# State space layer: decay tiles made earlier, one copy of B, C and the step rows, and four norm steps and two MLP steps moved to other turns

## The chip, the cores and the metric

The kernel runs on one core of one Trainium2 chip. A core has five engines that work side by side, each through its own queue in order: TensorE (PE, matrix products), VectorE (DVE), ScalarE (ACT), GpSimd (POOL) and SyncE (SP, which here issues transfers). They wait for one another through semaphores. An instruction that waits holds up everything behind it on its own engine. The metric is the time of one execution in microseconds (us) on the device; less is better. The kernel before took 11207.35 us in the median of three runs (11202.88 to 11211.71).

## The reference

The program is a network of four layers, each of a mixer and a feed-forward part. The change lies in the mixer of the third layer, a state space (Mamba) block followed by a small MLP. For an image of 4 x 64 x 128 x 128 values the reference computes, cut to what matters:

```python
mu = mean(xf); var = mean(square(xf - mu))
xn = (xf - mu) * rsqrt(var + LN_EPS)                 # norm over 64 channels
xi, z = split(xn @ in_proj_w.T)                      # 2 x 128 channels
xs = silu(causal_conv4(xi) + conv_b)
x_dbl = xs @ x_proj_w.T                              # 4 step, 16 B and 16 C rows
dt = softplus(x_dbl[..., :4] @ dt_proj_w.T + dt_proj_b)
def step(h, t):                                      # 128 channels x 16 states
    h = exp(dt_t * A) * h + (dt_t * x_t) * B_t
    return h, sum(h * C_t over states)
y = (scan of step) + xs * D
out = (y * silu(z)) @ out_proj_w.T
h1 = gelu(out @ fc1_w.T + fc1_b)                     # 128 -> 512, along the width
result = h1 @ fc2_w.T + fc2_b                        # 512 -> 128
```

## The kernel before, in words

The function `l2_conv` (line 2302) does this layer. The 4 images are taken as 2 pairs; the partitions hold two images of 64 channels, or, in the scan, two states of 64 channels. A sequence of 16384 positions is cut in 32 chunks of 512 positions (`L`, four columns of the image), so that there are 64 chunks in all. A chunk has T = 32 units (two images, 16 tiles of one state pair each). One unit is worked on in one turn of the main loop, and the loop goes over 2048 units in order. For each unit t:

- `decay` (line 2767) makes exp(dt A) on ACT into a tile `da`, three turns ahead; five such tiles exist.
- `spread` (line 2776) is a PE product that copies two rows of B over the partitions into a bank of PSUM, once for two units, three turns ahead, in odd turns t. There are four banks. A bank is used again for the input of the same units, so a spread waits for an earlier scan.
- `inputs` (line 2810) multiplies on DVE, one turn ahead, dt x by the spread B. Units 16 and 17 of every chunk are apart (`APART`): their B comes by a transfer, their product is made on POOL five turns ahead (`inputs_apart`, line 2805), their decay goes to a PSUM bank.
- `one_state` (line 2816) runs the scan over 512 positions on DVE, and the product `gs` with C on POOL.
- `summed` (line 2832) adds the products of two units in PSUM with PE, five turns later.

All else of a chunk is put in by turn numbers. `at(turn, step)` enters a step in a list; in each turn, after the unit's own work, the steps of that turn are issued. The order of issue is the order on PE, ACT, DVE and POOL (`manual_schedule`); SP's order follows from the framework. For chunk n, `norm` counts its turns from T(n-2), `project` from T(n-1), `leave` from T(n+1). So within the 32 turns of one chunk, steps of three other chunks run too, and turn numbers can be compared modulo 32.

- `norm` (line 2478): `scale`, `centre` (PE takes the mean away), `square` (ACT copies the result and squares it), `mean2` (PE sums the squares), `root` (ACT), `newton` (POOL refines the reciprocal root), `back` (PE spreads it, 8 products), `kept` (ACT copies it), `done` (POOL multiplies).
- `project` (line 2549): `conv`, `gate_in`, `silu`, then `bcr` (PE makes B three times, which gives with the products of `minus` a split in three bf16 parts, C, and the four step rows; all in one PSUM tile), `bcr_out` (three copies on ACT), `c_out` (transfers of B and C rows to memory), `steps` (PE, turn 15), `parts` (ACT, turn 16), `exp`, `one_more` (17), `log`, `lost` (18), `size` and `scaled` (POOL), and `twice` (transfers that lay dt and dt x out for the units).
- `leave` (line 2688): `sums` (DVE), `project_out`, `projected`, `layer1`, `hidden`, `gelu`, `layer2`, `put`.

Two PSUM names have one buffer each: `pa` (two banks wide) is shared by the convolution, the gate, B and C, the steps and both halves of layer1; `pn` is shared by the norm's products, project_out and layer2. A step that takes one of these must wait until the step before it has been copied out.

In the code and in the profile the functions and lines are:

Of the kernel before, what the change touches and what calls it, by code (L numbers as in the profile page):

```python
# [22 lines left out]
P = 128  # L23
# [2278 lines left out]
def l2_conv(env, x, out, prm):  # L2302
# [15 lines left out]
    with ExitStack() as ctx:  # L2318
# [7 lines left out]
        def load(name, shape, src):  # L2326
            t = cp.tile(shape, F32, name=name)
            nc.sync.dma_start(t, src)
            return t
# [54 lines left out]
        nc.vector.tensor_scalar(minus_i, env.ident[0 : 2 * N, 0 : 2 * N], -1.0, None, ALU.mult)  # L2384
        both = cp.tile([P, H], F32, name="both")
        nc.vector.tensor_add(both, env.ident[:, 0:H], env.ident[:, H:P])
        dtw = load("dtw", [R, D], prm["dt_proj_wT"])
        dtb = load("dtb", [P, 1], prm["dt_proj_b"].unsqueeze(1))
        am = cp.tile([P, S // 2, 2], F32, name="am")
        for i in range(2):  # L2390
# [27 lines left out]
        def at(turn, *steps):  # L2418
            turns.setdefault(turn, []).extend(steps)
# [4 lines left out]
        def tile_of(box, key, shape, name=None, bufs=2, dt=F32, pool=None):  # L2424
            box[key] = (pool or sb).tile(shape, dt, name=name or key, bufs=bufs)
            return box[key]
# [51 lines left out]
        def norm(n, t0):  # L2478
            g, w0 = chunks[n]
            x_ = boxes[n]  # L2480

            def scale(js):
                r, k = x_["rows"]
                if 0 in js:
                    tile_of(x_, "xn", [P, 3 + L], bufs=3)
                for j in js:
                    nc.scalar.activation(
                        x_["xn"][:, 3 + j * C : 3 + j * C + C], r["xt"][:, k + j, :], AF.Identity,
                        bias=r["nb"][:, k + j : k + j + 1], scale=r["rs16"][:, k + j : k + j + 1],
                    )  # L2490

            def centre():
                nc.tensor.matmul(tile_of(x_, "pm", [P, L], "pn", 1, pool=p1), less, x_["xn"][:, 3:], start=True, stop=True)

            def square():
                nc.scalar.copy(x_["xn"][:, 3:], x_["pm"])
                nc.scalar.activation(tile_of(x_, "sq", [P, L], "sq", 1), x_["pm"], AF.Square)

            def mean2():
                pv = tile_of(x_, "pv", [P, NW, 2], "pn", 1, pool=p1)  # L2500
                for q in range(NW):
                    nc.tensor.matmul(pv[:, q, :], x_["sq"][:, q * C : q * C + C], each, start=True, stop=True)

            def root():
                v, rs = tile_of(x_, "v", [P, NW, 2]), tile_of(x_, "rs", [P, NW, 2])
                nc.scalar.activation(v, x_["pv"], AF.Identity, bias=env.eps5)
                nc.scalar.activation(rs, v, AF.Ln)
                nc.scalar.activation(rs, rs, AF.Exp, scale=-0.5)

            def newton():  # L2510
                v, rs, t = x_["v"], x_["rs"], tile_of(x_, "r2", [P, NW, 2])
                nc.gpsimd.tensor_tensor(t, rs, rs, ALU.mult)
                nc.gpsimd.tensor_tensor(t, t, v, ALU.mult)
                nc.gpsimd.tensor_scalar(t, t, 0.5, -1.5, ALU.mult, ALU.add)
                nc.gpsimd.tensor_tensor(rs, rs, t, ALU.mult)

            def back():
                pr = tile_of(x_, "pr", [P, L], "pn", 1, pool=p1)
                for q in range(NW):
                    for b in range(2):  # L2520
                        nc.tensor.matmul(
                            pr[b * H : b * H + H, q * C : q * C + C], x_["rs"][:, q, b : b + 1].to_broadcast([P, H]),
                            env.ident, start=True, stop=True,
                        )

            def kept():
                nc.scalar.copy(tile_of(x_, "rt", [P, L], bufs=1), x_["pr"])

            def done():
                xn = x_["xn"]  # L2530
                if w0 == 0:
                    nc.gpsimd.memset(xn[:, 0:3], 0.0)
                else:
                    nc.gpsimd.tensor_copy(xn[:, 0:3], boxes[n - 1]["xn"][:, L : L + 3])
                nc.gpsimd.tensor_tensor(xn[:, 3:], xn[:, 3:], x_["rt"], ALU.mult)

            at(t0 - 2, lambda: scale((0, 1)))
            at(t0, lambda: scale((2, 3)))
            at(t0 + 3, centre)
            at(t0 + 4, square)  # L2540
            at(t0 + 5, mean2)
            at(t0 + 6, root)
            at(t0 + 8, newton)
            at(t0 + 11, back)
            at(t0 + 12, kept)
            at(t0 + 13, done)


        def project(n, t0):
# [52 lines left out]
            def bcr_out():  # L2602
                ps = x_["ps"]
                nc.scalar.copy(tile_of(x_, "bt", [3 * N, 2, L], dt=BF16), ps[0 : 3 * N])
                nc.scalar.copy(tile_of(x_, "bc", [2 * N, 2, L], bufs=1), ps[0 : 2 * N])
                nc.scalar.copy(tile_of(x_, "r", [R, 2, L], bufs=1), ps[3 * N : 3 * N + R])

            def c_out():
                for b in range(2):
# [13 lines left out]
            def steps():  # L2623
                pu = tile_of(x_, "pu", [P, 2, L], "pa", 1, pool=pa)
                for b in range(2):
                    nc.tensor.matmul(pu[:, b, :], dtw, x_["r"][:, b, :], start=True, stop=True)

            def parts():
                pu = x_["pu"]
# [58 lines left out]
        def leave(n, t0):  # L2688
# [7 lines left out]
            def project_out(b):  # L2696
                po = tile_of(x_, "po", [P, NW, H], "pn", 1, pool=p1)
                for j in range(NW):
                    nc.tensor.matmul(po[:, j, :], x_["y%d" % b][:, j * C : j * C + C], wo, start=True, stop=True)

            def projected(b):
                nc.scalar.copy(tile_of(x_, "o%d" % b, [P, NW * H], bufs=1), x_["po"].rearrange("c w h -> c (w h)"))

            def layer1(b):
                pf = tile_of(x_, "pf%d" % b, [P, F, NW * H], "pa", 1, pool=pa)
                for k in range(F):
                    nc.tensor.matmul(pf[:, k, :], f1[:, k, :], x_["o%d" % b], start=True, stop=True)  # L2707

            def hidden(b):
                gl = tile_of(x_, "gl%d" % b, [P, F, NW * H], bufs=1)  # L2710
                for k in range(F):
                    nc.scalar.activation(gl[:, k, :], x_["pf%d" % b][:, k, :], AF.Identity, bias=b1[:, k : k + 1])  # L2712
# [24 lines left out]

            at(t0 - S + LAG, lambda: sums(0))
            at(t0 + LAG, lambda: sums(1))
            at(t0 + 9, lambda: project_out(0))  # L2740
            at(t0 + 10, lambda: projected(0))
            at(t0 + 13, lambda: project_out(1))
            at(t0 + 14, lambda: projected(1))
            at(t0 + 18, lambda: layer1(0))
            at(t0 + 19, lambda: hidden(0))
            at(t0 + 21, lambda: layer1(1))
            at(t0 + 22, lambda: hidden(1))
            at(t0 + 24, gelu)
            at(t0 + 28, lambda: layer2(0, 0))
            at(t0 + 29, lambda: layer2(0, 1))  # L2750
# [13 lines left out]
        def apart(t):  # L2764
            return t % T // 2 * 2 in APART

        def decay(t):
            x_, b, s, _ = unit(t)
            da = bank(t, t % 2) if apart(t) else sb.tile([P, L], F32, name="da", bufs=5)
            nc.scalar.activation(da, x_["dt%d" % b][:, s % 2, :], AF.Exp, scale=am[:, s : s + 1])  # L2770
            live["da", t] = da

# [72 lines left out]
        with tc.manual_schedule(engines={E_.PE, E_.Activation, E_.DVE, E_.Pool}):  # L2845
            base_table()
            for n in range(0, len(chunks), NG):
                statistics(n, T * (n - 3))
            for n in range(len(chunks)):
                norm(n, T * (n - 2))  # L2850
                project(n, T * (n - 1))
                leave(n, T * (n + 1))
            for t in range(-4 * T, units + 2 * T):
                if 0 <= t + 3 < units:
                    decay(t + 3)
                if 0 <= t + 3 < units:
                    if (t + 3) % 2 == 0 and not apart(t + 3):
                        spread(t + 3)
                if 0 <= t + 10 < units and t % 2 == 0 and apart(t + 10):
                    fetch_b(t + 10)  # L2860
                if 0 <= t + 5 < units and apart(t + 5):
                    inputs_apart(t + 5)
                if t % QU == 2 and 0 <= t + 6 < units:
                    fetch(t + 6)
                if 0 <= t + 1 < units and not apart(t + 1):
                    inputs(t + 1)
                if 0 <= t < units:
                    one_state(t)
                for step in turns.pop(t, ()):
                    step()  # L2870
                if 0 <= t - LAG < units and (t - LAG) % 2 == 1:
                    summed(t - LAG)
# [697 lines left out]
```

## Time and profile before

| what | value |
|---|---|
| median of three runs | 11207.35 us |
| the profiled execution | 11202.36 us, its span 11200.5 us |
| stretch of the scans, span time 6333 to 10198 us | 3865 us, 64 chunks |
| DVE, POOL, PE, ACT busy in that stretch | 3692, 3508, 3381, 3175 us |
| mean granted TensorE clock in that stretch | 0.89 |
| ACT copies of B and C, of the step rows (L2605, L2606) | 1005 and 1007 ns each |

How to read it: the table by stretches gives for each stretch its length, then the busy time of PE, weight loads, DVE, ACT and POOL (with the number of instructions), the granted clock, the share of the transfer engines and GB/s. A list of waits has engine, tile and line of the one that waits, who released it, the sum in us, how many times, and the longest. The order in time has the start, the length, engine, line, operation, what is written from what, and in brackets the idle time of the engine just before it and what ended it. Starts are in us from the beginning of the span. The page merges neighbouring instructions of one kind (x8 is eight of them).

### The profile page before, as it was taken

The numbers are of one execution on the slowest core, as the hardware profiler recorded it, in microseconds if no ns is written. First come the engines' busy times: TensorE is split into PE (matmuls) and PEld (weight loads), VectorE is DVE, ScalarE is ACT, GpSimd is POOL, SyncE is SP. The second block draws the span as 40 slices with busy tenths as digits, with TensorE's granted clock in tenths as the row PEclk, the third lists the DMA queues.
The fourth block names the chain that finished last, engine by engine and source line by source line (L and its number), as shares of the span: only waits on it lengthen the run. The fifth ranks groups of instructions, "written<-read, shape, count | busy, mean of one in ns | idle before, by whom it ended". The sixth has DMA issues, their size and how long they took to land. (4 is left out here: it accounts for less than half of the span.)

```text
span 11200.5 us, 114412 instructions
## 1 busy us (share of the span) xinstructions
PE 6448.2 (58%) x33010; PEld 3781.1 (34%) x33010; DVE 9431.5 (84%) x14943; ACT 7408.7 (66%) x10451; POOL 5992.4 (54%) x5674
## 2 busy tenths in 40 slices
PE   7777686000000000003999688888888888887665
PEld 5665454000000000002898333333333333334342
DVE  7567646999999999998778599999999999997455
ACT  4244443788886777765555488888888888885443
POOL 1000025899992000001455499999999999894222
PEclk8887798555555555556999789889988989898877
DMA  6312246111111111112111254554554545543534
GB/s 195 107 36 48 56 160 159 51 58 56 59 58 54 57 54 56 53 45 61 47 56 47 70 126 119 127 126 118 131 123 121 128 122 123 129 116 108 193 132 169
DMA packets 806489, 1080.31 MB, mean 96 GB/s; under 512 B 245612, under 2 KB 462927, under 8 KB 792271
## 3 DMA queue, kind: packets, MB, share of 16 engines
q1 hardware_dynamic: 761918, 946.59, 30.6%
q0 software_dynamic: 34368, 124.14, 3.3%
q8 instruction: 266, 4.36, 0.2%
q14 instruction: 385, 3.15, 0.1%
q10 hardware_dynamic: 9552, 2.08, 0.1%
HBM read 699.16 MB, written 255.91 MB: 85 GB/s over the span
## 5 line engine op out<-in xcount | busy, mean ns | idle before, releaser
L2827 POOL TENSOR_TENSOR gs<-hist,cc 128x512 f32<-128x512 f32 x2048 | 2570.8, 1273 | 268.5 <-DVE hist L2822 200.9
L2822 DVE TENSOR_TENSOR_SCAN hist<-da,state,bs 128x512 f32<-128x512 f32 x1860 | 2360.0, 1271 | 48.2 <-ACT da L2770 47.0
L1698 PE MATMUL pm<-ident,m 128*1 128x128 f32 x1 | 0.4, 372 | 3193.0 <-DVE m L1696 3193.0
L2814 DVE TENSOR_TENSOR bs<-dx,bs 128x512 f32<-128x512 f32 x1920 | 1299.3, 677 | 159.9 <-PE bs L2780 110.9
L1506 POOL TENSOR_TENSOR diff<-key 128x2048 f32<-128x2048 f32 (+11 forms) x364 | 1384.0, 3851 | 81.8 <-DVE key L1511 75.5
L2770 ACT ACTIVATE da<-dt,am 128x512 f32<-128x512 f32 x1920 | 1294.5, 715 | 38.2 <-DVE hist L2822 29.7
L2838 PE MATMUL py<-gs,both 128*64 128x512 f32 x4096 | 1212.9, 672 | 1.4 <-POOL gs L2827 1.3
L1698 PEld LDWEIGHTS pm<-ident,m 128*1 128x1 f32 x1 | 0.1, 79 | 3193.1 <-issue 3193.1
L1936 POOL IOTA row<- 72x1 int32 x1 | 0.2, 230 | 1770.4 <-ACTq L1873 1770.4
L1528 ACT COPY keep<-rank 128x1536 int16<-128x1536 int16 (+11 forms) x364 | 612.8, 1686 | 437.7 <-DVE rank L1530 389.0
L1504 ACT COPY low<-key 128x2048 f32<-128x2048 f32 (+11 forms) x364 | 627.7, 1725 | 313.6 <-DVE key L1511 276.5
L1529 DVE COPY_PREDICATED rank<-back,rank 128x1536 int16<-128x1536 uint8 (+11 forms) x364 | 781.7, 2147 | 16.7 <-ACT keep L1528 16.7
L1530 DVE COPY_PREDICATED rank<-back,keep 128x1536 int16<-128x1536 uint8 (+11 forms) x364 | 777.8, 2137 | 12.5
L1511 DVE TENSOR_TENSOR key<-low,key 128x2048 f32<-128x2048 f32 (+11 forms) x364 | 744.5, 2045 | 12.4
L1510 DVE TENSOR_TENSOR key<-low,key 128x2048 f32<-128x2048 f32 (+11 forms) x364 | 749.1, 2058 | 2.4 <-ACT low L1504 2.4
L1507 ACT ACTIVATE turned<-diff 128x2048 int8<-128x2048 f32 (+11 forms) x364 | 600.4, 1699 | 8.4 <-POOL diff L1506 8.4
L1519 ACT ACTIVATE back<-turned 128x3072 uint8<-128x3072 int8 (+12 forms) x182 | 582.5, 3200 | 0.0
L2249 PE MATMUL pe<-ew,xg 128*128 128x128 f32 x4096 | 506.6, 278 | 0.0
L2249 PEld LDWEIGHTS pe<-ew,xg 128*128 128x128 f32 x4096 | 491.0, 193 | 19.2 <-issue 2.9
L1031 POOL DMA_DIRECT2D state<-zz x16 | 18.5, 1156 | 856.2 <-DVE zz L1021 615.8
L2780 PE MATMUL bs<-bt,pick 96*128 96x512 bf16 x960 | 394.5, 411 | 120.0 <-DVE hist L2822 117.5
L2707 PE MATMUL pa<-o,f 128*128 128x256 f32 x1024 | 361.5, 514 | 107.5 <-ACT gl L2712 93.4
(858 smaller groups left out, 17618.0 us busy)
## 6 DMA issues: line engine op xcount, KB each, us to landing
cc<-cd SPq DMA_DIRECT2D x1024, 256.0 KB
xt<-state SPq DMA_DIRECT2D x64, 1024.0 KB
dt<-w SPq DMA_DIRECT2D x512, 128.0 KB
dx<-up SPq DMA_DIRECT2D x512, 128.0 KB
xo<-state SPq DMA_DIRECT2D x128, 256.0 KB
state<-xo POOLq DMA_DIRECT2D x128, 256.0 KB, 3.0
xl<-in_L_ffn_weight SPq DMA_DIRECT2D x32, 1024.0 KB
tk<-in_x SPq DMA_DIRECT2D x32, 512.0 KB
```

Of the source, the lines that this page charges most:

```text
L1504: nc.scalar.copy(c, l)
L1506: nc.gpsimd.tensor_sub(d, lo[part], hi[part])
L1510: nc.vector.tensor_tensor(lo[part], c, hi[part], ALU.min)
L1511: nc.vector.tensor_tensor(hi[part], c, hi[part], ALU.max)
L1529: nc.vector.copy_predicated(l, t, h)
L1530: nc.vector.copy_predicated(h, t, kv)
L2249: T.matmul(w["pe"][:, j, :], w["xg"][:, q, j, :], ew[:, q, :], start=False, stop=(j == 3 and q == E - 1))
L2770: nc.scalar.activation(da, x_["dt%d" % b][:, s % 2, :], AF.Exp, scale=am[:, s : s + 1])
L2814: nc.vector.tensor_mul(live["db", t], x_["dx%d" % b][:, s % 2, :], live["bs", t - s % 2])
L2822: nc.vector.tensor_tensor_scan(h, live.pop(("da", t)), live.pop(("db", t)), 0.0 if first else state[b][:, s : s + 1], ALU.mult, ALU.add,)
L2827: nc.gpsimd.tensor_tensor(gs, h, live.pop(("cc", t)), ALU.mult)
L2838: nc.tensor.matmul(x_["py%d" % b][h * H : h * H + H], both, live.pop(("gs", t - 1 + h)), start=False, stop=(s == S - 1),)
```

## The change

It does six things.

1. The tile pool of decays has eight tiles instead of five, and a decay is issued five turns ahead instead of three. The two units apart stay at three.
2. `bcr_out` makes two copies instead of three. The tile `bc` takes all 100 rows of the PSUM tile (B three times and the four step rows, where it took 64), and `r` is gone.
3. The weights of `steps` are laid out for those 100 rows: `dtw` has 96 rows of zeros, written by DVE, above its four. `steps` contracts over 100 rows instead of 4.
4. In `norm`: `square` goes from turn 4 to 5, `mean2` from 5 to 9, `root` from 6 to 10, `newton` from 8 to 12, `back` from 11 to 13, `kept` from 12 to 14, `done` from 13 to 16.
5. In `leave`: the two `project_out` go from turns 9 and 13 to 11 and 15, the two `projected` from 10 and 14 to 12 and 16.
6. In `leave`: the two `layer1` go from turns 18 and 21 to 17 and 20, the two `hidden` from 19 and 22 to 18 and 21.

```diff
-        dtw = load("dtw", [R, D], prm["dt_proj_wT"])
+        dtw = cp.tile([3 * N + R, D], F32, name="dtw")
+        nc.vector.memset(dtw, 0.0)
+        nc.sync.dma_start(dtw[3 * N :], prm["dt_proj_wT"])
...
-            at(t0 + 4, square)
-            at(t0 + 5, mean2)
-            at(t0 + 6, root)
-            at(t0 + 8, newton)
-            at(t0 + 11, back)
-            at(t0 + 12, kept)
-            at(t0 + 13, done)
+            at(t0 + 5, square)
+            at(t0 + 9, mean2)
+            at(t0 + 10, root)
+            at(t0 + 12, newton)
+            at(t0 + 13, back)
+            at(t0 + 14, kept)
+            at(t0 + 16, done)
...
-                nc.scalar.copy(tile_of(x_, "bc", [2 * N, 2, L], bufs=1), ps[0 : 2 * N])
-                nc.scalar.copy(tile_of(x_, "r", [R, 2, L], bufs=1), ps[3 * N : 3 * N + R])
+                nc.scalar.copy(tile_of(x_, "bc", [3 * N + R, 2, L], bufs=1), ps[0 : 3 * N + R])
...
-                    nc.tensor.matmul(pu[:, b, :], dtw, x_["r"][:, b, :], start=True, stop=True)
+                    nc.tensor.matmul(pu[:, b, :], dtw, x_["bc"][:, b, :], start=True, stop=True)
...
-            at(t0 + 9, lambda: project_out(0))
-            at(t0 + 10, lambda: projected(0))
-            at(t0 + 13, lambda: project_out(1))
-            at(t0 + 14, lambda: projected(1))
-            at(t0 + 18, lambda: layer1(0))
-            at(t0 + 19, lambda: hidden(0))
-            at(t0 + 21, lambda: layer1(1))
-            at(t0 + 22, lambda: hidden(1))
+            at(t0 + 11, lambda: project_out(0))
+            at(t0 + 12, lambda: projected(0))
+            at(t0 + 15, lambda: project_out(1))
+            at(t0 + 16, lambda: projected(1))
+            at(t0 + 17, lambda: layer1(0))
+            at(t0 + 18, lambda: hidden(0))
+            at(t0 + 20, lambda: layer1(1))
+            at(t0 + 21, lambda: hidden(1))
...
-            da = bank(t, t % 2) if apart(t) else sb.tile([P, L], F32, name="da", bufs=5)
+            da = bank(t, t % 2) if apart(t) else sb.tile([P, L], F32, name="da", bufs=8)
...
-                if 0 <= t + 3 < units:
+                if 0 <= t + 5 < units and not apart(t + 5):
+                    decay(t + 5)
+                if 0 <= t + 3 < units and apart(t + 3):
                     decay(t + 3)
```

## The prediction

> **What bounds the kernel now.** I read the page, the table by stages, the waits of each engine in the state space stage, and then one group of 32 turns (span time 7545 to 7604 us) engine by engine in order of time.
>
> ```profile
> span 11200.5 us, 114412 instructions
> 6333.00:10198.00 3865.00, 3380.72 (x13418) 1432.78 (x13417) 3692.49 (x4336) 3175.37 (x4769) 3508.41 (x3504) 0.89 0.50 123
> DVE bs L2814 <- PE bs L2780: 110.9, 100, 3.0
> DVE hist L2822 <- ACT da L2770: 48.0, 54, 3.1
> PE pn L2502 <- ACT sq L2497: 163.8, 61, 5.1
> PE pa L2707 <- ACT gl L2712: 91.7, 54, 2.6
> ```
>
> The second line is the stage the change touches: 3865 us, in which DVE is busy 3692.5 (third pair), POOL 3508 and PE 3381. DVE bounds it. Its idle 172.5 us are nearly all two waits: for a spread B row from PE (110.9) and for a decay from ACT (48.0, with 1.0 in another form). So no change of order can win more than 172 us here. PE's own waits come next: it stands for the squares of the norm (163.8) and for the hidden copy that frees the only `pa` bank pair (91.7).
>
> DVE, POOL, PE and ACT in the typical group:
>
> ```profile
> 7567.60 1.27 DVE L2822 TENSOR_TENSOR_SCAN hist<-da,state,bs 128x512 f32<-128x512 f32 x1
> 7574.67 0.68 DVE L2814 TENSOR_TENSOR bs<-dx,bs 128x512 f32<-128x512 f32 x1
> 7585.88 0.68 DVE L2814 TENSOR_TENSOR bs<-dx,bs 128x512 f32<-128x512 f32 x1
> ```
> ```profile
> 7562.98 0.20 POOL L2512 TENSOR_TENSOR r<-rs 128x8 f32<-128x8 f32 x1
> 7563.83 0.20 POOL L2515 TENSOR_TENSOR rs<-rs,r 128x8 f32<-128x8 f32 x1
> 7565.47 1.27 POOL L2827 TENSOR_TENSOR gs<-hist,cc 128x512 f32<-128x512 f32 x1 [0.21 <-DVE hist L2822]
> 7566.70 1.28 POOL L2808 TENSOR_TENSOR db<-dx,bb 128x512 f32<-128x512 f32 x1
> 7569.29 1.27 POOL L2808 TENSOR_TENSOR db<-dx,bb 128x512 f32<-128x512 f32 x1
> 7570.52 2.51 POOL L2827 TENSOR_TENSOR gs<-hist,cc 128x512 f32<-128x512 f32 x2
> ```
> ```profile
> 7437.05 1.87 PE L2502 MATMUL pn<-each,sq 128*128 128x2 f32 x8 [5.08 <-ACT sq L2497]
> 7442.68 0.61 PE L2780 MATMUL bs<-bt,pick 96*128 96x512 bf16 x1
> 7568.24 1.09 PE L2521 MATMUL pn<-ident,rs 128*64 128x128 f32 x16
> 7577.42 1.99 PE L2707 MATMUL pa<-o,f 128*128 128x256 f32 x8 [0.47 <-ACT up L2631]
> 7584.86 3.65 PE L2707 MATMUL pa<-o,f 128*128 128x256 f32 x8 [2.60 <-ACT gl L2712]
> ```
> ```profile
> 7576.26 1.11 ACT L2631 ACTIVATE up<-pa,dtb 128x1024 f32<-128x1024 f32 x1
> 7583.27 1.54 ACT L2712 ACTIVATE gl<-pa,b 128x256 f32<-128x256 f32 x4
> ```
>
> and the granted clock, last but two in each row of the table by stretches:
>
> ```profile
> 7437.00:7443.80 6.80, 6.75 (x16) 3.07 (x17) 5.51 (x7) 3.75 (x9) 4.77 (x7) 0.50 0.28 69
> 7585.00:7588.40 3.40, 3.40 (x9) 2.69 (x10) 3.40 (x5) 1.64 (x3) 3.40 (x2) 0.51 0.50 154
> ```
>
> DVE: 7567.60 is scan 12, 7574.67 the first input after the two apart turns (input 18), 7585.88 input 24. A turn is 1.77 us. POOL: `newton` (four operations, 7562.98 to 7564.03) follows gs 8; 7565.47 is gs 10, the two `db` rows are the apart inputs of units 16 and 17, the last row is gs 12 and gs 13. PE: `back` at 7568.24 waits for nothing. The two layer1 rows are the same eight matmuls, 1.99 us and, after a wait of 2.60, 3.65, at a granted clock of 0.51. After the wait of 5.08 (another group) the clock was 0.50 for 6.8 us. PE has little reserve: a spread goes into a bank that the scan one turn earlier has just left, and its input follows two turns later.
>
> **What the change removes.** Decays five turns ahead: the waits for `da` (49.0) go. ACT is busy 3175 of 3865 and each decay gains two turns, 3.5 us, over a worst wait of 3.1. The tables' decay inputs (`dt`) must then land 3.5 us sooner; that wait was 0.4 us in all. At most ACT waits 3.5 us a group, behind five decays in hand (8.9 us): nothing on DVE. Squares at 5, `mean2` at 9: in the typical group `sq` ended at 7556.6, now one more decay lies ahead of it (7557.2), and PE asks at about 7562, behind spread 12. The wait of 163.8 goes, and the late spreads behind it. I count all 110.9 as gone: together -160. On PE `mean2` now stands behind `bcr`, so ACT's `bt` comes sooner.
>
> The third copy (`r`, 63 x 1.007 = 63 us) leaves ACT, which is no bound; PE's wait for it (55.0) shrinks by a microsecond a group, in a stretch where PE then has time. The 100-row `bc` costs what the 64-row copy did (1005 ns; the 96-row `bt` took 1008). `steps` over 100 rows instead of 4: 652 ns in its own row, 680 for the 128-row `xp` product, so 0 to 4 x 28 ns a group; I take 0. The memset of `dtw` stands in the prologue, on a DVE with 1.2 us of work in the 60 us before the first scan: 0, at most the 3 us of one DMA landing behind it.
>
> SP's order of loads: `twice` waits for POOL's `size`, which hangs on `steps`; `cc` fetches stand behind it. Since DVE itself comes later by then (below), I take 0; the bound is one group's later `steps`, 1.04 us a group.
>
> **What it adds: `back` waits for `newton`.** `newton` moves from turn 8 to 12, `back` only from 11 to 13. On POOL turns 11 and 12 hold the two apart inputs. So `newton` now stands behind gs 12: gs 12 is half of the x2 row and ends at 7571.8; plus 1.05 is 7572.8. This can't be much earlier: gs 10 waited for its scan. PE gets to `back` after spread 14 (from the end of scan 10, about 7565.25), project_out 1.0, `minus` 0.53, summed 1.0: 7568.2. So PE stands 4.7 us, each group. Behind it in PE's queue: `back` 1.03, summed 1.01, spread 18 0.39: 2.4 us at full clock, ending at 7575.3. DVE asks at 7574.67: 0.7 us of stall. But the row with the 5.08 us wait shows what follows such a wait: `mean2` to spread took 7437.05 to 7443.29, 6.2 us, for work that takes 3.35 elsewhere (0.92 + 1.03 + 1.01 + 0.39). At that ratio, 1.86, spread 18 ends at 7577.4: 2.7 us. I take 2.7, since 4.7 is near 5.08; ends 0.7 and 2.7.
>
> **And spread 24 falls behind layer1(1).** Call E the end of spread 18. Then project_out(1), moved here from turn 13, 1.04, and `steps` 1.91; `parts` on ACT end at E + 5.1. layer1(0) (1.93), summed, spread 22: E + 8.5. On ACT, from the end of `parts`: decay 0.61, exp 1.08, one_more 1.09 + 1.06, decay 0.61, hidden(0) 1.54: E + 11.1. PE waits 2.6 us for it, as it did before. But layer1(1) now stands in turn 20, ahead of spread 24 (turn 21), which used to be done by then. Layer1(1) at the slow row's 3.44, summed 1.01, spread 0.39: E + 16.0; at the fast row's 1.93, E + 14.5. DVE wants spread 24 at 11.2 after spread 18 (7585.88 - 7574.67). Stall 4.8, or 3.3 with the fast row. I take 4.8: the same wait of 2.6 in the same place had the slow row.
>
> **Sum.** 2.7 + 4.8 = 7.5 us in 62 groups (the last two have no norm): +465, less 160: +305. The profiled execution took 11202.4 (its span and 1.9 around it), 5 below the median of 11207.35; on the median, 11512. I say 11510.
>
> The Trainium skill, "TensorE: Matmul & The Clock Gate" (Part 1, and the closing table), says that about 3.4 us of idle halve the clock, and about 3.4 us of work bring it back: a rule against the new wait of 4.7 us. The trace agrees for 5.08, not for 2.60, where matmuls were already slow. By the rule layer1(1) would stay fast: 62 x 6.0 - 160 = +212, an estimate of 11419 from that page and these rows.
>
> **Rivals.**
> - *Full clock* (0.20): the waits come, matmuls stay fast. 62 x (0.7 + 3.3) - 160 = +88: 11295. For it: the stage's mean granted clock is 0.89, so most of it runs full. Against: both long waits shown were followed by 0.50 and 0.51.
> - *Longer half clock* (0.12): also project_out(1) (+1.0), and summed and spread after layer1(1) (+1.4), run slow: 9.9 us, +454: 11660. For: after the 5.08 wait `bcr` too took 2.89 for 1.88.
> - *Faster* (0.10): `newton` is there when PE asks, so spread 18 ends at its earliest, end of scan 14 + 0.39 = 7572.8, and layer1(1) stays fast: spread 24 at 7587.3, 1.4 us of stall, 62 x 1.4 - 160 = -73: 11134; -160 (11047) if that goes too. It decides below 160 / 62 = 2.6 us a group. POOL would need 4.7 us in turns 9 to 12; it has the 1.05 of the old `newton`, but its products wait for scans.
> - *No difference* (0.03): stalls of about 2.6 that cancel.
>
> **Chances.** My forecast 0.55, own range 11400 to 11600. Under 0.2% (22 us) this kernel's runs can't tell a change: slower 0.87, same 0.03, faster 0.10. The range leaves out the faster cases and the end of the longest: 11220 to 11650.
>
> **What would show it.** Right: PE waiting at `back` for POOL's `rs`, 4 to 5 us, 62 times (some 280 us); the wait for `sq` and DVE's for `da` near 0; DVE's wait for PE's `bs` from 111 to some 450, at inputs 18 to 24. Wrong: no wait at `back`; DVE's wait for `bs` under 160.

## The result, and the profile after

The changed kernel takes 11540.08 us in the median of six runs (11529.77 to 11557.36), the kernel before, run beside it, 11205.83 us (11198.96 to 11213.73). The ratio is 1.0299, with a 95% interval of 1.0286 to 1.0313: slower by 3%.

Profile of the changed kernel: the first line of the page, the stage of the scans in the table by stretches (columns as before: length, PE, weight loads, DVE, ACT, POOL, granted clock, DMA share, GB/s), and the lists of waits of DVE and PE.

```profile
span 11528.0 us, 114269 instructions
```
```profile
6305.50:10512.40 4206.90, 3383.14 (x13398) 1445.12 (x13398) 3681.65 (x4327) 3122.81 (x4711) 3521.07 (x3501) 0.89 0.45 113
```
```profile
DVE y L2695 <- PE py L2839: 328.1, 64, 6.4
DVE bs L2815 <- PE bs L2781: 191.8, 170, 3.9
```
```profile
PE pn L2523 <- POOL rs L2517: 245.6, 62, 5.5
PE pa L2708 <- ACT gl L2713: 158.5, 64, 2.6
```

From the first scan to the end of the last the stage took 3865.4 us before and takes 4206.9 now: 341.5 more, with DVE's work the same (3692 and 3682 us busy). DVE's waits in that stage were 172.5 us, none of them for `py`; now the two lines alone make 519.9, of which 6 lie behind the last scan. The waits for `da` and of PE for `sq` are gone from the lists, as forecast. In their place stand PE's wait at `back` (L2523) for POOL's `newton`, 62 times, and DVE's wait for the summed products (`y`, L2695), which the kernel before has once, 5.6 us, behind the last scan. The profiled executions differ by 327.4 us: +341.5 in the stage, -17.9 ahead of the first scan, +3.9 behind the last. Of the 17.9, 11.5 lie ahead of this layer, where nothing was changed; so a profile's time can't be read closer than some ten microseconds, and for the parts below I also give the length of the stage.

The same place of a group as shown for the kernel before, now in the changed kernel (scan 0 at 7635.9, scan 12 at 7657.7), in order of time, POOL, then PE, then DVE:

```profile
7659.42 1.27 POOL L2809 TENSOR_TENSOR db<-dx,bb 128x512 f32<-128x512 f32 x1
7660.65 1.27 POOL L2828 TENSOR_TENSOR gs<-hist,cc 128x512 f32<-128x512 f32 x1
7662.73 0.20 POOL L2517 TENSOR_TENSOR rs<-rs,r 128x8 f32<-128x8 f32 x1
```
```profile
7657.64 1.08 PE L2839 MATMUL py<-gs,both 128*64 128x512 f32 x4
7662.98 1.97 PE L2523 MATMUL pn<-ident,rs 128*64 128x128 f32 x16 [4.26 <-POOL rs L2517]
7664.74 1.92 PE L2839 MATMUL py<-gs,both 128*64 128x512 f32 x4
7666.59 0.53 PE L2781 MATMUL bs<-bt,pick 96*128 96x512 bf16 x1
...
7677.89 3.78 PE L2708 MATMUL pa<-o,f 128*128 128x256 f32 x8 [2.56 <-ACT gl L2713]
7681.60 1.97 PE L2839 MATMUL py<-gs,both 128*64 128x512 f32 x4
7683.51 0.61 PE L2781 MATMUL bs<-bt,pick 96*128 96x512 bf16 x1
```
```profile
7667.16 0.70 DVE L2815 TENSOR_TENSOR bs<-dx,bs 128x512 f32<-128x512 f32 x1 [2.27 <-PE bs L2781]
7683.65 0.69 DVE L2695 TENSOR_TENSOR y<-z,py 128x512 f32<-128x512 f32 x1 [6.40 <-PE py L2839]
```

`newton` ends behind the second apart product and gs 12, at 7662.93, 5.2 us after the start of scan 12. PE has been idle for 4.26 us by then; `back` then takes 1.97 us for the 1.09 of before, and input 18 stands 2.27 us. Layer1(1) starts after 2.56 us of idle, takes 3.78, and behind it summed 20 and spread 24. But it is not input 24 that stands: it is `y`, one step ahead of it on DVE.

The granted clock, third from the end, in the two stretches behind these waits of the changed kernel:

```profile
7663.00:7666.40 3.40, 3.40 (x20) 1.98 (x20) 1.89 (x2) 1.34 (x3) 3.40 (x3) 0.50 0.30 66
7677.90:7683.00 5.10, 5.10 (x12) 2.81 (x12) 0.00 (x0) 4.00 (x8) 5.10 (x5) 0.50 0.42 97
```

It is 0.50 in both, and in the second DVE does nothing at all.

### The profile page after: what moved, and what is told of

Same layout as the page of the kernel before. It is cut to its first block, busy times and chain, and to the rows that moved or that the text cites. A ratio compares the mean times of both kernels' runs of the same rounds, so it can differ in the third digit from the quotient of the medians.

```text
span 11528.0 us, 114269 instructions
## 1 busy us (share of the span) xinstructions
PE 6456.9 (56%) x33010; PEld 3799.4 (33%) x33010; DVE 9423.8 (82%) x14944; ACT 7350.6 (64%) x10387; POOL 6006.8 (52%) x5674
## 5 line engine op out<-in xcount | busy, mean ns | idle before, releaser
L2815 DVE TENSOR_TENSOR bs<-dx,bs 128x512 f32<-128x512 f32 x1920 | 1313.4, 684 | 232.0 <-PE bs L2781 191.8
L2708 PE MATMUL pa<-o,f 128*128 128x256 f32 x1024 | 335.3, 484 | 208.9 <-ACT gl L2713 158.5
```

What stands on the lines that cost most here:

```text
L2815: nc.vector.tensor_mul(live["db", t], x_["dx%d" % b][:, s % 2, :], live["bs", t - s % 2])
```

## The experiments

Theory: two stalls, each with its own cause: `newton` behind the apart inputs in POOL's order, with `back` one turn later on PE; and layer1(1) ahead of summed 20. Both are made dearer by the half clock. Rivals: one of the two alone does it; the decays ahead or the 100-row copy cost the time; the clock is no part of it.

**back17: PE asks for the root later.**

```diff
-            at(t0 + 13, back)
-            at(t0 + 14, kept)
-            at(t0 + 16, done)
+            at(t0 + 17, back)
+            at(t0 + 18, kept)
+            at(t0 + 20, done)
```

> The changed kernel with back at turn 17, kept at 18, done at 20; newton stays at 12, so PE asks four turns later. Theory (two stalls, each its own): the wait of PE for POOL's rs (246 us, 62 times) goes, and with it DVE's stalls at inputs 18 and 20 (2.07 + 0.92 us a group); layer1(1) still stands ahead of summed 20, for which the sums wait: of its 5.9 us a group 3.3 to 4.8 stay, since PE reaches it sooner but hidden(0) does too. 62 x (4.2 to 5.7) less than 11540: 11190 to 11280. Rival (only the place of layer1 costs, the wait at back lies in time that PE has left): 11500 or more. Rival (decays ahead or the 100-row copy cost it): 11540.

Measured: 11298.68 us (before beside it 11217.52; ratio 1.0073, 1.0057 to 1.0090). PE's wait at `back` is gone, DVE's wait for `bs` fell from 191.8 to 96.4, for `y` from 328.1 to 178.8. Both rivals fall; the time is 19 us above the forecast. `y` fell too, though layer1 was not moved back: PE waits 1.7 us in the mean ahead of layer1(1) instead of 2.5, and those eight products then run at 2.03 us instead of 3.24 (means over the groups, from the trace's start times).

**layer_old: layer1 where it was.**

```diff
-            at(t0 + 17, lambda: layer1(0))
-            at(t0 + 18, lambda: hidden(0))
-            at(t0 + 20, lambda: layer1(1))
-            at(t0 + 21, lambda: hidden(1))
+            at(t0 + 18, lambda: layer1(0))
+            at(t0 + 19, lambda: hidden(0))
+            at(t0 + 21, lambda: layer1(1))
+            at(t0 + 22, lambda: hidden(1))
```

> The changed kernel with layer1 and hidden at their turns of before (18, 19, 21, 22). Theory: the stall at the sums goes (DVE y for PE py, 328 us); the wait at back stays with its 3.0 us a group; layer1(1) then stands ahead of spread 26, behind which 2 to 3 us of stall return: 62 x 5.0 to 6.0 instead of 9.0: 11330 to 11370. Rival (the wait at back costs nothing by itself): 11050 to 11150, below the kernel before. Rival (decays ahead or the copy): 11540.

Measured: 11374.44 us (ratio 1.0142, 1.0125 to 1.0159). DVE's wait for `y` is 5.5 us, that for `bs` 319.8, and PE's wait at `back` stays (221.4). This is 4 us above the forecast, and both rivals fall: one stall is worth 166 us by itself, the other stays. Of the 328 us for `y`, 128 come back as waits for `bs`, most of them (1.3 us a group) at input 26, behind layer1(1) in its old place.

**both: the two edits together.**

> Both of the two last edits: back at 17 and layer1 where it was before. Theory: both stalls go, 0.2 to 1.7 us a group stay at spread 26, and what the change removes (160 us) stays removed: 11040 to 11110, faster than the kernel before by 1 to 1.5 percent. Rival (decays ahead or the copy cost time): above 11206.

Measured: 11274.11 us (ratio 1.0055, 1.0039 to 1.0072): a miss. The two edits together gave 266 us, hardly more than `back` at 17 alone (241), and the kernel is still slower than before. That is where the rival had it; the next run rules that rival out. DVE's wait for `bs` is 194.7. By turns, 1.7 us a group stand at input 26, 0.6 at input 20, 0.8 at inputs 2 and 4. So `back` at 17 was no clean way of taking its wait away. A likely reason is that `done` at 20 comes between the links of POOL's chain that leads to dt x; the run with `newton` at 10 and layer1 in its old place, below, fits this, but no run moves `done` alone.

**no_turns: of the change only the decays ahead and the one copy, on the kernel before.**

```diff
-            da = bank(t, t % 2) if apart(t) else sb.tile([P, L], F32, name="da", bufs=5)
+            da = bank(t, t % 2) if apart(t) else sb.tile([P, L], F32, name="da", bufs=8)
...
-                if 0 <= t + 3 < units:
+                if 0 <= t + 5 < units and not apart(t + 5):
+                    decay(t + 5)
+                if 0 <= t + 3 < units and apart(t + 3):
                     decay(t + 3)
...
-                nc.scalar.copy(tile_of(x_, "bc", [2 * N, 2, L], bufs=1), ps[0 : 2 * N])
-                nc.scalar.copy(tile_of(x_, "r", [R, 2, L], bufs=1), ps[3 * N : 3 * N + R])
+                nc.scalar.copy(tile_of(x_, "bc", [3 * N + R, 2, L], bufs=1), ps[0 : 3 * N + R])
```

> The kernel before with the eight decay tiles five turns ahead and the one copy alone; no step changes its turn. Theory: DVE's wait for da (49 us) goes, a little of it comes back as waits for spread rows, and the copy that is left out helps the stretch behind bcr: 11140 to 11190. Rival (decays ahead or the 100-row copy are what made the changed kernel slow): 11300 or more.

Measured: 11161.27 us (ratio 0.9955, 0.9938 to 0.9971). The rival falls: what the change adds in decays and copies makes the kernel faster; the loss is in the turns.

**warm: PE works while it waits.**

```diff
                 pr = tile_of(x_, "pr", [P, L], "pn", 1, pool=p1)
+                for _ in range(3):
+                    nc.tensor.matmul(pr, less, x_["xn"][:, 3:], start=True, stop=True)
```

> The changed kernel, and ahead of back three products of 128x512 (less times xn) into the same PSUM tile, which back overwrites: PE works for about 3.1 of the 4.3 us in which it stood. The result is the same. Theory (the half clock is part of the price): after the wait, back to spread 18 took 4.14 us in the typical group; at full clock 2.35. Everything behind follows 1.8 us sooner: 62 x 1.8 = 111 less than 11540, so 11430 (11400 to 11470), with a granted clock near 1.0 behind back. Rival (only the wait itself costs; the clock does not follow PE's idle time, or the price is paid again at layer1): 11520 or more.

Measured: 11370.69 us beside 11200.99 (ratio 1.0159, 1.0142 to 1.0176): 169 us less than the changed kernel by the medians, 157 by the ratios, with more work on PE. That is beyond the forecast of 111, and 29 us under its range. The products behind the wait, from `back` to spread 18, in this kernel:

```profile
7680.14 1.09 PE L2525 MATMUL pn<-ident,rs 128*64 128x128 f32 x16 [1.95 <-POOL rs L2517]
7681.06 1.77 PE L2841 MATMUL py<-gs,both 128*64 128x512 f32 x4
7682.76 0.61 PE L2783 MATMUL bs<-bt,pick 96*128 96x512 bf16 x1
```

Here `back` runs at 1.09 and the clock falls only behind it (0.67 granted from 7680.1 to 7683.4); over all groups the way from the start of `back` to the end of spread 18 takes 2.46 us in the mean, against 4.09 in the changed kernel (from the trace's start times). Layer1(1) went from 3.24 to 2.48 too, though its own wait stayed as long (2.5 and 2.6 us in the mean). Of the gain, DVE's wait for `bs` gives 122 us (69.5 instead of 191.8) and that for `y`, behind layer1(1), 48 (280.2 instead of 328.1). So the clock is more than half of what the first wait costs in all (245 us, next run, where 64 of it are `y`), and the rival falls.

**newton10: one number of the changed kernel.**

```diff
-            at(t0 + 12, newton)
+            at(t0 + 10, newton)
```

> The changed kernel with one number changed: newton at turn 10 instead of 12, so that on POOL it stands ahead of the two apart inputs and of gs 11 and gs 12; back stays at 13. Theory (it is the place in POOL's order): newton ends 5.2 us sooner, at about the start of scan 12, PE's wait at back goes (246 us to under 20), stalls at inputs 18 and 20 go; the stall at the sums stays as with back at 17: 11240 to 11300. Rival (newton waits for root on ACT, so its turn changes little): 11450 to 11540.

Measured: 11294.81 us (ratio 1.0080, 1.0063 to 1.0096), as forecast. On POOL and PE of one group (scan 12 at 7583.15):

```profile
7583.14 0.20 POOL L2517 TENSOR_TENSOR rs<-rs,r 128x8 f32<-128x8 f32 x1
7583.30 1.28 POOL L2809 TENSOR_TENSOR db<-dx,bb 128x512 f32<-128x512 f32 x1
```
```profile
7583.14 1.08 PE L2839 MATMUL py<-gs,both 128*64 128x512 f32 x4
7584.05 1.04 PE L2523 MATMUL pn<-ident,rs 128*64 128x128 f32 x16
```

`newton` ends 0.2 us after the start of scan 12, 5.0 us sooner, `back` waits for nothing, and 245 us are gone by moving four operations of 1.05 us past two apart products and two `gs` on POOL. The rival falls. What is left is the other stall: DVE waits 264.1 us for `y` and 33.6 for `bs`.

**newton10_layer_old: the same, and layer1 where it was** (the two edits above together).

> As e6_newton10, and layer1 and hidden at their turns of before. The run with back at 17 and layer1 where it was before missed its forecast (11274 instead of 11040 to 11110): of its stalls 1.7 us a group lay at input 26, behind layer1(1), 0.6 at input 20, behind project_out(1) at turn 15, 0.8 at inputs 2 and 4 and some at loads. Theory: the 0.8 and part of the loads came from done at turn 20, which pushes POOL's chain to dt x; with done at 16 they go, the 1.7 and 0.6 stay: 11180 to 11240. Rival (they come from the decays ahead): 11270.

Measured: 11162.32 us (ratio 0.9958, 0.9943 to 0.9973), 18 us under the forecast. With both stalls gone by clean means the change as a whole is faster than the kernel before. The rival falls; what stays (122.6 us of waits for `bs`) lies at input 26 above all, 1.5 us a group.

**copy_alone: the kernel before with the one copy only** (the last lines of the diff of no_turns, and the wider `dtw`).

> The kernel before with the one copy of B, C and step rows alone (dtw of 100 rows); five decay tiles, three turns ahead, no step moved. Theory (the copy costs and gives next to nothing, and the 49 us of the run with both edits come from the decays): 11190 to 11215. Rival (the copy gives the gain, since PE's wait for it, 55 us, lies on the path): 11150 to 11170. Rival (100 rows make steps or the copy dearer): above 11225.

Measured: 11158.4 us (ratio 0.9954, 0.9940 to 0.9967). My theory fell here: the copy alone gives as much as copy and decays. DVE's waits, first in this kernel, then in the one with decays and copy:

```profile
DVE bs L2815 <- PE bs L2781: 59.6, 64, 1.9
DVE hist L2823 <- ACT da L2771: 55.0, 47, 3.1
```
```profile
DVE bs L2815 <- PE bs L2781: 118.9, 72, 4.5
```

The copy takes 51 us off the wait for `bs`, and the time is the one that the first rival named. By turns, 31 of the 44 us by which the stage is shorter lie at input 22, whose spread stands behind layer1(0) on PE. The eight products of layer1(0) took 3.0 us in the mean in the kernel before and take 2.1 here. Two stretches of the kernel before (columns as above) show what slowed them:

```profile
7455.34:7458.75 3.41, 3.41 (x11) 1.01 (x10) 3.41 (x5) 1.82 (x3) 3.41 (x5) 1.00 0.13 31
7458.75:7462.17 3.42, 2.80 (x8) 1.89 (x7) 3.42 (x4) 3.39 (x5) 3.37 (x3) 0.50 0.62 152
```

In the first PE is busy throughout, and yet the clock is 0.50 in the second, where layer1(0) starts and takes 3.78 us. The first holds `steps`, over 4 rows. In the scans of the kernel before the clock falls behind 39 such stretches of 3.41 us with PE busy for more than 90%, and `steps` stands in every one. In the twelve other kernels, all with `steps` over 100 rows, there is no such fall. So the 100 rows, with zeros for weights, kept the clock where 4 rows did not. PE's wait for the third copy (55.0) is gone too; no run separates the two.

The decays then do take away the 55.0 for `da`; but 59 come back as waits for `bs`. At input 10 DVE now stands 1.3 us a group instead of 0.4: it is no longer held at scan 5 (0.8 us a group), and comes that much sooner to a spread that stands behind `mean2`, while PE's wait there for the squares is about what it was (185 and 180 us). (The decays alone were not run: eight tiles fit only in the room that `r` leaves.)

**mean2_7: decays, copy, and of the norm only `mean2` and what hangs on it, on the kernel before.**

```diff
-            at(t0 + 5, mean2)
-            at(t0 + 6, root)
-            at(t0 + 8, newton)
+            at(t0 + 7, mean2)
+            at(t0 + 8, root)
+            at(t0 + 9, newton)
```

> The kernel before with the eight decay tiles five turns ahead, the one copy, and of the norm only mean2 at 7, root at 8 and newton at 9; square, back, kept, done, project_out and layer1 keep their turns. Theory: PE no longer stands for the squares ahead of spread 10 (184 us of PE's waits in the run without moved turns, 1.4 us a group of DVE stall at input 10), newton is still ahead of the apart inputs: 62 x 1.4 less than 11161: 11060 to 11110, the fastest so far. Rival (the stall moves to the next place): 11140 to 11170.

Measured: 11087.79 us beside 11200.99 (ratio 0.9896, 0.9880 to 0.9913), as forecast and faster than both kernels. DVE waits 60.1 us for `bs`, and not for `da`.

**mean2_7_no_decays: the same with five tiles, three turns ahead.**

> The kernel before with the one copy and mean2 at 7, root at 8, newton at 9; five decay tiles three turns ahead as before. In the runs so far the copy alone gave what the copy and the decays gave together (11158 and 11161): DVE's 55 us of waits for da went, and as much came back at input 10, behind mean2, which waits for the squares that the decays now stand ahead of. Theory (the decays are worth their 50 us once mean2 no longer stands ahead of spread 10): this kernel is 45 to 60 us slower than e8_mean2_7 (ratio 0.9896): ratio to the kernel before 0.9935 to 0.995, 11130 to 11150 beside 11205. Rival (the decays give nothing, mean2 alone makes e8_mean2_7): ratio 0.989 to 0.991, about 11090.

Measured: 11159.96 us beside 11219.36 (ratio 0.9946, 0.9932 to 0.9960), as forecast by the ratio. By the length of the stage:

| kernel | stage, us |
|---|---|
| before | 3865.4 |
| copy | 3821.2 |
| copy, mean2 at 7 | 3804.4 |
| copy, decays | 3811.6 |
| copy, decays, mean2 at 7 | 3756.5 |

In these profiles `mean2` takes 17 us off the stage that the copy leaves, the decays 10, both together 65. The 17 and the 10 can't be told from nothing: the ratios of these kernels (0.9954 with the copy, 0.9946 and 0.9955) have intervals that overlap. The 65 can (0.9896). Neither stall goes alone: without the decays DVE still waits 53.2 us for `da`, without `mean2` it waits behind the squares instead.

**mean2_7_warm: one product more ahead of layer1(1).**

```diff
+                if b == 1:
+                    fill = tile_of(x_, "fill", [P, L], "pn", 1, pool=p1)
+                    nc.tensor.matmul(fill, less, f2.rearrange("p f c -> p (f c)"), start=True, stop=True)
                 pf = tile_of(x_, "pf%d" % b, [P, F, NW * H], "pa", 1, pool=pa)
```

> As e8_mean2_7, and ahead of layer1(1) one product of 128x512 into an unused PSUM tile, so that PE does not stand for the whole 2.2 us there. Theory (the half clock is part of what is left): layer1(1) goes from 3.1 to about 2.1 us behind that wait, and most of the stall at input 26 (0.85 us a group) goes: 30 to 50 us under e8_mean2_7, that is 11040 to 11060 beside a kernel before of 11201. Rival (the wait for hidden(0) itself sets it, or the extra product delays the spread rows where there was no wait): 11080 or more.

Measured: 11077.37 us beside 11212.74 (ratio 0.9878, 0.9863 to 0.9893). Its interval overlaps that of mean2_7, so the gain of the extra product is not shown in the time; the stage is 12 us shorter (3744.7), the stall at input 26 went from 0.85 to 0.42 us a group. That is less than the 30 to 50 us forecast. Either way these two versions, 1.0 to 1.2% faster than the kernel before, are the best of the study.

## Why the prediction was right, and where it was not

- *What is added, `back` behind `newton`: right.* Forecast 4.7 us of wait in 62 groups, some 280 us; measured 245.6, 62 times, 4.0 in the mean and 4.26 in the group shown. `newton` ended 5.2 us after scan 12, as worked out. Stall at input 18: forecast 2.7, between 0.7 at full clock and 2.7 at the ratio of the 5.08 us row; it was 2.27 in the group shown (1.9 in the mean), at a clock of 0.50. The run with the root made sooner removes it, the run with products in the wait shows the clock's part.
- *Spread 24 behind layer1(1): right in its cause, mis-sized, and at the wrong place.* "DVE wants spread 24 at 11.2 after spread 18": but summed 20 is held up by layer1(1) as well, and DVE asks for its result sooner. In the kernel before that row is

```profile
7583.52 0.66 DVE L2694 TENSOR_TENSOR y<-z,py 128x512 f32<-128x512 f32 x1
```

  that is 8.85 after input 18 (7574.67), 2.4 us before input 24. In the changed kernel summed 20 ends 16.45 after spread 18 (7683.57 less 7667.12), where I had worked out 15.6. The stall is 7.3 us (0.29 + 0.61 + 6.40; 6.4 in the mean over the groups), not 4.8. For the same reason the sign I had named for the profile, 450 us of DVE's wait for `bs`, was wrong: 191.8, and 328.1 for `y`. The rule is plain: of everything that stands behind a waiting instruction the one that is asked for first sets the price.
- *What is removed: near in its sum, wrong in its parts.* The waits for `da` did go. But I had put all 110.9 us of waits for `bs` at the late squares. Only 26 lie at input 10, behind `mean2`; 42 lay at input 26 and 29 at input 22. Input 22 waits as long as before (0.43 us a group, 0.46 then), and the wait at 26 is gone only because DVE now stands at `y` ahead of it: with layer1 at its old turns it is back, at 1.3 to 1.6 us a group. And "the third copy leaves ACT, which is no bound", at 0, was wrong: by itself the copy is worth 0.46% (11158 beside 11213), most of it at input 22. For `steps` over 100 rows I asked only what it costs itself; what it did was to keep the clock for layer1(0). Nor are the decays' 49 theirs alone: without `mean2` moved, they come back one wait further on.
- *The sum.* DVE's waits in the stage are 514 us now, where I had 465 coming, and were 172.5, where I had 160 going. Against this stand 17.9 us ahead of the first scan, unforeseen. 11540 for 11510, inside the range; that it is so near is partly luck: the 49 us that were missing from what is added are offset in good part by the other two.
- *The rivals.* Full clock (11295) falls by the rows of 0.50. Longer half clock: summed and spread behind layer1(1) did run slow (1.97 and 0.61, where 1.08 and 0.39 are the rule), project_out(1) did not (1.00). Faster would have needed `newton` 4.7 us sooner: one turn number later in the study did just that, and with layer1 back in its place the result was faster.
- *The Trainium skill.* "TensorE: Matmul & The Clock Gate" (Part 1) holds that about 3.4 us of idle halve the clock. Here the clock was 0.50 behind a wait of 2.56 us, and it had fallen 1.8 us into that wait (last section); the sum by that rule, 11419, was 121 us low.

## What to carry to other kernels

Where each engine works through its queue in order, a step's turn is only as good as its place in the queue of the engine that feeds it: look at what stands ahead of the producer (here two apart products and two `gs`, 1.27 us each) before you move the consumer up to it. When a wait moves, list everything behind it on that engine, and price it by the one that is asked for first. And a gain that hides a wait may only show once the next wait in line is gone too: on top of the copy, decays and `mean2` each gave nothing that stands clear of the scatter, and 65 us together.

## What the runs showed that I had not expected

Work put into a wait can make a kernel faster. Three extra products of 128x512 in each group cost nothing and saved some 160 us of 11540, since PE then kept its clock: from the start of `back` to the end of spread 18 2.46 us instead of 4.09.

The length of a wait alone does not say whether the clock falls. Ahead of layer1(1) PE waits 1.7 us in the mean both with `back` at 17 and in the run without moved turns, and the eight products take 2.03 us in the one and 2.91 in the other; with layer1 in its old place it waits 2.7 us, and they take 2.64. In these traces the granted clock changes only at steps of 3.41 us. Two steps of the changed kernel, around the start of layer1(1):

```profile
7673.73:7677.15 3.42, 1.60 (x7) 0.29 (x5) 2.81 (x3) 3.39 (x6) 1.30 (x1) 1.00 0.00 0
7677.15:7680.56 3.41, 2.67 (x6) 2.19 (x7) 0.10 (x1) 3.41 (x6) 3.41 (x4) 0.50 0.00 0
```

PE is idle from 7675.33 to 7677.89, but the clock is 0.50 from 7677.15 on, 1.8 us into the wait. Ahead of `back` PE is idle from 7658.72 on, and the clock is 0.50 from 7660.09, 1.4 us into the wait. In the stage of this kernel 175 steps at full clock were followed by half the clock; PE was busy in them 32% of the time in the median and 64% at most. Behind the 777 others the clock stayed full; PE was busy in them 95% in the median and 45% at least. So in this kernel the clock went with how much PE had done in a step, and a wait of the same length can lie in one step or be shared by two.
